# A graph transformer kernel: the first batch's rows of layers 1 and 2 picked at the end of the layer ahead, and half of its gathers dropped

## The chip, the cores and the metric

The kernel runs on one core of a Trainium2 chip. The metric is the device time of one execution in microseconds (us); lower is better. A core has a matrix engine (PE), a vector engine (DVE), a scalar engine (ACT), a general engine (POOL, which here does nothing but issue indirect gathers) and a queue engine (SP, which here issues most of the plain transfers, in the order written).

## The reference

Three layers of a graph transformer over N = 6250 nodes of width D = 64 and E = 206250 edges, which are sorted by destination node. Cut to what matters:

```python
for i in range(3):
    q = x @ Wq[i] + bq[i]; k = x @ Wk[i] + bk[i]; v = x @ Wv[i] + bv[i]
    e = edge_attr @ We[i]
    alpha = sum(q[dst] * (k[src] + e), -1) / sqrt(D)
    p = exp(alpha - segment_max(alpha, dst)[dst])
    w = p / segment_sum(p, dst)[dst]
    x = segment_sum((v[src] + e) * w[:, None], dst) + x @ Ws[i] + bs[i]
    x = relu(x)
    if i < 2: x = layer_norm(x, gamma[i], beta[i])
return layer_norm(x0 + log_softmax(x))
```

Each layer needs the row of `x` of each edge's source node, and these rows are known only when the layer ahead has finished its nodes.

## The kernel before

**Tiling.** The nodes stand in 49 blocks of 128, and the blocks in groups of four, the last two being group 44 (three blocks) and group 47 (two). The edges are cut into batches of 3072: four chunks of 768, each of six tiles of 128. There are 67 full batches and one small one; a batch is worked on as one unit, `u` = 0 to 67, and NU = 68. `chunks[layer, u].turn(j)` transposes chunk j on PE (L1754), `line.scores(u, h)` makes the scores (PE L1767, DVE maximum L1781 and L1794), `weights` the softmax weights (ACT L1800, PE L1814), `line.sums(u)` the weighted sums (PE L1826), and `line.store()` copies them out of PSUM (ACT L1833) and stores them to one of two tables `part` (SP L1839, four small transfers per unit).

**Node work.** `finish(layer, g, n)` takes a group of blocks whose sums are complete: it loads both tables' rows (`both`, L1552) and the skip term (`sk`, L1557), joins the tables (`mm` L1565, `w` L1574 and L1577, PE L1581), adds and normalises (`y` L1606, the statistics L1530 and L1532, L1545), stores the rows of the next layer's x (`x<-y`, SP L1614), and goes on in `project` to the next layer's queries and skip term (PE L1498, L1503 and L1512, DVE `skip` L1514). It is a generator: each `close_up()` moves every group in work one step on, and does a step of `reload` first, so node work lies between the edge work in the order that the program writes it. That order is the order on every engine; nothing is rearranged later.

**Source rows.** They come into `feat` in two ways. POOL gathers one tile of 128 rows per indirect transfer (`gather`, L610); in layers 1 and 2 the first batch's gathers read their indices from `src_b`, the others from a `gate`, a copy of indices on ACT (L642) that is made when a buffer has come free. Or the row is picked: PE multiplies a one-hot matrix `hot` (made on DVE from `keys`, L1382, with `which` L1371) with a resident copy `parts` of x (`Picker.batch`, L1453), DVE takes the result out of PSUM (`evacuate`: L1408 and three L1410), and ACT swaps two pieces (L1393 to L1395). The nodes stand in eight ranges for this; each is loaded through `start` (SP L1344) and split into a high and a low part (`split`: ACT cast L1315, DVE subtract L1316). Batches of layers 1 and 2 have 24 rows of tiles, of which 12 are picked and 12 gathered; picks reach ranges 0 to 5 only. `LEAD` says how many batches at a layer's start are not picked:

```python
PICKS = ((8,), (12,), (12,))
LEAD = (3, 1, 1)
```

**The end of a layer.** After the loop over u come, in writing, the last two units: turns of unit 66, its scores, `sums(65)`, a store, unit 67's turn and scores, `sums(66)`, a store, `sums(67)`, a store, with `line.refill(u)` (which hands unit u's `feat` buffer to a later batch and issues its 768 KB load of edge values, SP L579) between them. Then come the loads of keys for batches 0 to 2 of the next layer (`decode`, 384 KB each, L1913), the loads for its unit 0 (`q`, `featT`, `fourth`, `shade`), the rest of the node groups down to the store of group 47's rows, and only then the first gathers, which may read any row of x. Ranges that are not yet split follow last.

Of the kernel before, what the change touches and what calls it, by code (L numbers as in the profile page):

```python
# [11 lines left out]
F32 = mybir.dt.float32  # L12
# [9 lines left out]
P = 128  # L22
D = 64
L = 3
# [9 lines left out]
GS = 4  # L34
# [8 lines left out]
NW = 8  # L43
WT = 2
# [4 lines left out]
GC = 16  # L49
ROWS = 8  # L50
PICKS = ((8,), (12,), (12,))
LEAD = (3, 1, 1)
NH = WB // KB
AHEAD = 3

# [377 lines left out]
def main_path(  # L433
# [53 lines left out]
    nc = tc.nc  # L487
# [4 lines left out]
    REST = tiles - NT * LB * TC  # L492
    assert NT > LEAD[0] and REST <= TC
    NC = NT * LB + 1
# [31 lines left out]
    nodes = ctx.enter_context(tc.tile_pool(name="nodes", bufs=2))  # L526
# [13 lines left out]

    U0 = LEAD[0]
    STEP = -(-(N - WB * P) // (NW - 1))
# [18 lines left out]
    skS = [dram.tile([P, NB, D + 1], F32, name=f"skS{i}") for i in range(L)]  # L561
# [34 lines left out]
    def depth(n):  # L596

        return [(n // 2 + 1 - pair) // 2 for pair in range(LB // 2)]
# [32 lines left out]
    def await_turn(layer, k):  # L631

        pending.extend((layer, k, c) for c in range(batches[k][1]))
# [26 lines left out]
    for k in range(NK):  # L660
        n = min(P, NC - k * P)
# [96 lines left out]
    for k in range(NK):  # L758
        n = min(P, NC - k * P)
# [548 lines left out]
    held = []  # L1308
    lacking = []

    def split(w, y):

        at = w % HALF * WB
        here = parts[w // HALF][:, :, at : at + WB]
        nc.scalar.copy(here[:, 0], y)  # L1315
        nc.vector.tensor_tensor(here[:, 1], y, here[:, 0], ALU.subtract)  # L1316

    def range_of(layer, w):

        return xts[layer][w * STEP : w * STEP + WB * P, :].rearrange("(j p) d -> p j d", p=P)  # L1320
# [12 lines left out]

    def reload(layer):

        while held and (len(held) > 1 or not lacking):
            split(*held.pop(0))
        if not lacking:
            return
        w = lacking[0]  # L1340
        if all((layer - 1, g) in written for g, _ in groups if g * P < w * STEP + WB * P):
            lacking.pop(0)
            y = start[:, w % SLOTS * WB * D :][:, : WB * D].rearrange("p (j d) -> p j d", d=D)
            nc.sync.dma_start(y, range_of(layer, w))  # L1344
            held.append((w, y))
# [201 lines left out]
    def finish(layer, g, n):  # L1547

        at_end = g + n == NB
        both = nodes.tile([P, 2, GS, R], F32, name="both", bufs=1)  # L1550
        for h in range(2):
            nc.sync.dma_start(  # L1552
                both[:, h, :n, :],
                tables[h][g * P : (g + n) * P, :].rearrange("(j p) c -> p j c", p=P),
            )
        sk = nodes.tile([P, GS, D + 1], F32, name="sk", bufs=1)[:, :n]
        nc.sync.dma_start(sk, skS[layer][:, g : g + n, :])  # L1557
        xr = rows_of(g, n) if layer == L - 1 else None
        yield
        if not at_end and g + 2 * GS > NB:  # L1560
            for _ in range(3):
# [87 lines left out]
    def advance(those=None):  # L1649
        those = active if those is None else those  # L1650
        for g in list(those):
            if next(g, those) is those:
                those.remove(g)

    class Unit:
# [36 lines left out]
        def ask(self):  # L1692

            self.b = []
            for j in range(self.m):
                b = nc.values_load(
                    base[0:1, self.c + j : self.c + j + 1],
                    engines=(ENG.SP,),
                    min_val=0,
                    max_val=NB * P,  # L1700
                    skip_runtime_bounds_check_because="the least of a chunk's nodes, NB*128 at most",
                )
                self.b.append(b)
                nc.sync.dma_start(self.q[:, j * W : (j + 1) * W], qq[self.layer][:, ds(b, W)])
# [267 lines left out]
    def step(n=1):  # L1972
        for _ in range(n):
            advance()
# [3 lines left out]
    def close_up(n=1):  # L1978
        step(n)
        for _ in range(n):  # L1980
            advance(ending)
        if lacking or held:
            reload(current[0] + 1)
# [4 lines left out]
    serve()  # L1988
    for layer in range(L):
        line = Line(layer)  # L1990
        assert not picked(layer, 0)

        def free(u, j):
            lead = 2 * LB if not layer else min(2 * LB, LB + u)
            release(layer, u * LB + j + (0 if not layer else 1) + lead, nc.scalar.copy)

        picker = Picker(layer)
        for u in range(NU - 2):
            this = chunks[layer, u]
            picking = picker.batch(u + 1)  # L2000
            n = len(picker.picks(u + 1))
# [74 lines left out]
        more = layer + 1 < L  # L2076
# [3 lines left out]
        assert not picker.todo and not picker.hots  # L2080
        if more:
            current[0] = layer
            lacking.extend(range(NW))
            if not layer:
                early.close()
                psum.append(ctx.enter_context(tc.tile_pool(name="psum", bufs=1, space=bass.MemoryType.PSUM)))
                bank_of.update({"g": "p", "node": "a", "s1": "p", "w0": "s"})
                stock[0] = ctx.enter_context(tc.tile_pool(name="picks", bufs=2))
                parts.append(stock[0].tile([P, 2, HALF * WB, D], F32R, name="parts", bufs=1))
        u = NU - 2  # L2090
        full = chunks[layer, u]
        line.sums(u - 2)
# [23 lines left out]
        line.scores(u, 0)  # L2116
        line.scores(u, 1)
        line.sums(u - 1)
        line.refill(u - 1)
        line.store()  # L2120
        close_up()
        last.turn(0)
        last.uncode()
# [3 lines left out]
        line.scores(u + 1, 0)  # L2127
        line.scores(u + 1, 1)
        line.sums(u)
        line.refill(u)  # L2130
        line.store()
        close_up()
        line.weights(u + 1, 0)
        line.weights(u + 1, 1)
        close_up()
        line.sums(u + 1)
        line.refill(u + 1)
        line.store()
        close_up()
        if more:  # L2140
            decode(layer + 1, 0)
            decode(layer + 1, 1)
            decode(layer + 1, 2)
            ask(layer + 1, 0)
            chunks[layer + 1, 0].across()
            chunks[layer + 1, 0].shade()
# [4 lines left out]
        if more:  # L2151
            assert all((layer, g) in written for g, n in groups)
            for k in range(FB):
                if (layer + 1, k) not in loaded:
                    fetch(layer + 1, k)
                if k:
                    await_turn(layer + 1, k)
                else:
                    gather_all(layer + 1, k)
            while lacking or held:  # L2160
                reload(layer + 1)
            while ending:
                close_up()

# [44 lines left out]
```

## Time and profile before

| what | value |
|---|---|
| time, median of 3 runs | 4140.61 us (4136.73 to 4148.78) |
| the profiled execution | 4139.31 us, its span 4137.5 us |
| PE busy | 3364.6 us, 81% |
| DVE busy | 2977.8 us, 72% |
| POOL busy | 2827.9 us, 68% |
| ACT busy | 2351.6 us, 57% |
| mean granted PE clock | 0.933 |
| POOL idle between layers 0 and 1, and 1 and 2 | 59.04 us and 46.10 us |

A row of a timeline reads: start, duration (of the whole group when it has a count), engine, line and operation, output and inputs, the count, and in square brackets the idle time before it with what ended it. A row of the windows reads: the stretch, its length, busy us of PE, PE's weight loads (PEld), DVE, ACT and POOL, each with its count of instructions, then the granted PE clock, the busy share of the transfer engines and GB/s. In the rows of groups stand count, busy us, mean ns of one, and the idle time ahead of them with its releasers. "issue" is time in which an engine waited for nothing that the profile shows. SPq is SP's queue. Line numbers are those of the kernel before.

### The profile page before, as it was taken

Reading aid. Unit: us, or ns where it says so; the run is one execution under the profiler, and the core shown is the slowest. Engines: PE = TensorE matmul, PEld = TensorE weight load, DVE = VectorE, ACT = ScalarE, POOL = GpSimd, SP = SyncE. Lnnn points to the kernel's source line nnn. Section 1 sums busy time; section 2 is a strip of 40 time slices with the busy share of each in tenths; the row PEclk is TensorE's granted clock in tenths of the full one; section 3 lists DMA queues with packets and bytes.
Section 4 is the critical chain, followed back from the end, with each engine's and each line's share of the span. In section 5 each row is a group of like instructions: output and inputs, shape, how many; then the busy total and the mean of one; then the engine's idle time right before and its main releaser. Section 6 shows DMA issues by size and latency. Waiting matters only on the chain.

```text
span 4137.5 us, 105363 instructions
## 1 busy us (share of the span) xinstructions
PE 3364.6 (81%) x34183; PEld 2391.6 (58%) x34183; DVE 2977.8 (72%) x10306; ACT 2351.6 (57%) x6011; POOL 2827.9 (68%) x2774
## 2 busy tenths in 40 slices
PE   3889899999989899984778788888757878778776
PEld 1445555555555555553666666666646666666664
DVE  5677888888878888864667777777646667777775
ACT  0455565565656555563556556565635656666665
POOL 5467666666667666663777777777657777777774
PEclk9899999999999999996999999999969999999998
DMA  5667677666767666765677777777657677777774
GB/s 111 185 175 198 171 192 181 180 183 184 188 161 193 179 180 175 183 174 125 173 183 193 186 183 185 188 189 188 164 135 183 173 190 182 187 189 183 186 184 102
DMA packets 787997, 728.88 MB, mean 176 GB/s; under 512 B 487336, under 2 KB 612450, under 8 KB 787440
## 3 DMA queue, kind: packets, MB, share of 16 engines
q1 hardware_dynamic: 630436, 504.14, 47.6%
q0 software_dynamic: 88448, 90.75, 11.6%
q10 hardware_dynamic: 68556, 127.16, 8.7%
q8 instruction: 278, 4.55, 0.5%
q14 instruction: 279, 2.29, 0.2%
HBM read 562.78 MB, written 158.81 MB: 174 GB/s over the span
## 4 chain that ended last, share of the span: by engine, by line


## 5 line engine op out<-in xcount | busy, mean ns | idle before, releaser
L610 POOL DMA_INDIRECT feat<-x,gate x1592 | 1579.9, 992 | 485.4 <-issue 372.9
L610 POOL DMA_INDIRECT feat<-in_x,gate x1100 | 1175.4, 1069 | 652.6 <-ACT gate L642 323.5
L1453 PE MATMUL ps_x<-parts,hot 128*128 128x256 f32 x6336 | 941.8, 301 | 0.0
L1453 PEld LDWEIGHTS ps_x<-parts,hot 128*128 128x128 f32 x6336 | 841.8, 202 | 81.8 <-DVE feat L1410 62.5
L1757 ACT COPY featT<-ps_a 64x384 f32<-64x384 f32 x1320 | 627.1, 475 | 393.5 <-PE ps_a L1754 369.5
L1410 DVE COPY_PREDICATED feat<-which,ps_x 128x256 f32<-128x256 int32 (+1 forms) x1584 | 592.4, 374 | 54.3
L1408 DVE COPY feat<-ps_x 128x256 f32<-128x256 f32 (+1 forms) x528 | 187.7, 355 | 587.0 <-PE ps_x L1453 577.2
L1754 PE MATMUL ps_a<-ident,feat 128*128 128x128 f32 x2380 | 451.0, 289 | 176.2 <-DMA feat<-x,gate 139.7
L1101 DVE TENSOR_SCALAR hit<-ruler,pos 128x384 bf16<-128x384 f16 x1608 | 501.8, 324 | 30.3 <-PE ps_m L1121 30.2
L1754 PEld LDWEIGHTS ps_a<-ident,feat 128*128 128x128 f32 x2380 | 283.3, 144 | 385.7 <-issue 276.0
L1382 DVE TENSOR_SCALAR hot<-keys,rank 128x512 fp32r<-128x512 f16 (+1 forms) x1040 | 432.9, 482 | 9.1 <-DMA keys<-keyS 5.2
L1826 PE MATMUL ps_p<-feat,probT 128*32 128x128 f32 x6600 | 236.3, 295 | 91.4 <-ACT probT L1817 77.8
L1112 PE MATMUL ps_x<-hit,raw 128*64 128x384 bf16 x1608 | 293.8, 360 | 2.5 <-DVE hit L1101 2.2
L1112 PE MATMUL ps_x<-hit,rest 128*64 128x384 bf16 x1608 | 275.0, 338 | 0.0
L1112 PE MATMUL ps_x<-hit,end 128*64 128x384 bf16 x1608 | 274.2, 337 | 0.0
L1826 PEld LDWEIGHTS ps_p<-feat,probT 128*32 128x32 f32 x6600 | 193.6, 119 | 129.4 <-ACT probT L1817 102.9
L1767 PE MATMUL ps_s<-featT,q 128*32 128x384 f32 x1866 | 228.0, 496 | 11.6 <-DMA featT<-eaS 7.3
L1814 PE MATMUL ps_s<-ident,prob 128*128 128x128 f32 (+1 forms) x417 | 81.3, 307 | 191.6 <-ACT prob L1800 188.7
L1453 PE MATMUL ps_p<-parts,hot 128*128 128x256 f32 x992 | 163.8, 311 | 80.5 <-DVE feat L1410 73.5
L1800 ACT ACTIVATE prob<-prob,part 128x768 f32<-128x768 f32 x204 | 190.0, 931 | 68.7 <-DVE part L1794 60.1
L1453 PEld LDWEIGHTS ps_p<-parts,hot 128*128 128x128 f32 x992 | 137.1, 204 | 112.5 <-DVE feat L1410 91.8
L1833 ACT COPY part<-ps_p 128x128 f32<-128x128 f32 (+1 forms) x140 | 37.3, 267 | 244.9 <-PE ps_p L1826 239.8
(281 smaller groups left out, 5960.6 us busy)
## 6 DMA issues: line engine op xcount, KB each, us to landing
featT<-eaS SPq DMA_DIRECT2D x658, 192.0 KB
feat<-eaP SPq DMA_DIRECT2D x134, 768.0 KB
raw<-in_ea SPq DMA_DIRECT2D x536, 96.0 KB
eaS<-eT ACTq DMA_DIRECT2D x134, 384.0 KB
keys<-keyS SPq DMA_DIRECT2D x132, 384.0 KB
eaP<-feat ACTq DMA_DIRECT2D x128, 384.0 KB
shade<-maskS SPq DMA_DIRECT2D x198, 192.0 KB
fourth<-eaS SPq DMA_DIRECT2D x134, 192.0 KB
```

The source lines that it names most:

```text
L610: nc.gpsimd.indirect_dma_start(out=feat[:, c, t, 0], out_offset=None, in_=xts[layer][:, :], in_offset=bass.IndirectOffsetOnAxis(ap=index[: ...
L1101: nc.vector.tensor_scalar(hit, ruler, self.pos[:, at : at + 1], None, ALU.is_equal)
L1112: nc.tensor.matmul(self.px[j * D : (j + 1) * D, :HE], self.parts[2 * h + i].thirds[part][:, j, t * D : (t + 1) * D], self.hits[h, 2 * i + ...
L1382: nc.vector.tensor_scalar(hot[:, h], keys[self.layer, k][:, first : first + n], rank[:, h : h + 1], None, ALU.is_equal)
L1408: nc.vector.tensor_copy(found, px[:, :, :, 0])
L1410: nc.vector.copy_predicated(found, which[:, :, :, b].bitcast(I32).unsqueeze(3).to_broadcast([P, 2, m, D]), px[:, :, :, b],)
L1453: nc.tensor.matmul(px[:, t - t0, v].rearrange("p b d -> p (b d)"), hot[:, h, (2 * pair + v) * P : (2 * pair + v + 1) * P], those[:, i, b0 ...
L1754: nc.tensor.transpose(pt[:, t * P : (t + 1) * P], rows[:, 2 * t * D : 2 * (t + 1) * D], ident)
L1757: nc.scalar.copy(featT[:, :, h, :], pt[h * D : (h + 1) * D, : n * P].rearrange("d (i e) -> d i e", e=P))
L1767: nc.tensor.matmul(p_s[rows, :w], self.q[:, rows], self.featT[j][:, cols], start=True, stop=True)
L1800: nc.scalar.activation(self.prob[:n, : self.cols], self.prob[:n, : self.cols], AF.Exp, bias=neg, accum_out=self.part[:n, P + 1 : P + 2],)
L1826: nc.tensor.matmul(p_g[rows, :].rearrange("n (h d) -> n h d", h=2), self.probT[:, t, rows], batch[:, j, t], start=(t == 0), stop=(t == sel ...
```

## The change

`LEAD` becomes (3, 0, 0), so batch 0 of layers 1 and 2 is picked like the others: 12 of its 24 gathers go, and 48 pick matmuls with their hots, evacuations and swaps come in. They are made at the end of the layer ahead. The picker of the next layer is opened behind the store of unit 65's sums, which makes the first hots there; the keys of batches 0 and 1 are therefore loaded ahead of the last two units; and the picks are written out behind the store of the last sums. Of the eight ranges six are reloaded. `reload` splits at most one range per step. `refill` stands behind the stores, and the last two behind the very last store. In `finish`, `sk` is loaded ahead of `both`.

```diff
-LEAD = (3, 1, 1)
+LEAD = (3, 0, 0)
...
     def reload(layer):
-        while held and (len(held) > 1 or not lacking):
+        if held and (len(held) > 1 or not lacking):
             split(*held.pop(0))
...
     def finish(layer, g, n):
         at_end = g + n == NB
+        sk = nodes.tile([P, GS, D + 1], F32, name="sk", bufs=1)[:, :n]
+        nc.sync.dma_start(sk, skS[layer][:, g : g + n, :])
         both = nodes.tile([P, 2, GS, R], F32, name="both", bufs=1)
...
-        sk = nodes.tile([P, GS, D + 1], F32, name="sk", bufs=1)[:, :n]
-        nc.sync.dma_start(sk, skS[layer][:, g : g + n, :])
...
-        picker = Picker(layer)
+        if not layer:
+            picker = Picker(layer)
...
-            lacking.extend(range(NW))
+            lacking.extend(range(WT * max(depth(max(PICKS[layer + 1])))))
...
+            decode(layer + 1, 0)
+            decode(layer + 1, 1)
         u = NU - 2
...
         line.sums(u - 1)
+        line.store()
         line.refill(u - 1)
-        line.store()
+        if more:
+            picker = Picker(layer + 1)
+            picker.aim()
         close_up()
...
         line.sums(u)
-        line.refill(u)
         line.store()
...
         line.sums(u + 1)
-        line.refill(u + 1)
         line.store()
         close_up()
+        line.refill(u)
+        line.refill(u + 1)
         if more:
-            decode(layer + 1, 0)
-            decode(layer + 1, 1)
+            for _ in picker.batch(0):
+                pass
+            picker.flush()
             decode(layer + 1, 2)
...
-            while lacking or held:
-                reload(layer + 1)
```

Three places show how the order on the engines moves. The first is PE at the end of layer 0, between group 44's join (L1581) and its projection (L1512) and values (L1603); `hot_…` are the one-hot matrices of batch 0, one for each of three tile positions.

```order
 L1826 MATMUL ps_p<-feat,probT 32x128 x4
 L1581 MATMUL ps_a<-ident,w 128x128 x3
+L1453 MATMUL ps_x<-parts,hot_32669 128x256 x8
+L1453 MATMUL ps_x<-parts,hot_32672 128x256 x8
+L1453 MATMUL ps_x<-parts,hot_32675 128x256 x8
+L1453 MATMUL ps_x<-parts,hot_32669 128x256 x8
+L1453 MATMUL ps_x<-parts,hot_32672 128x256 x8
+L1453 MATMUL ps_x<-parts,hot_32675 128x256 x8
 L1512 MATMUL ps_a<-ws,xT 128x65 x4
 L1603 MATMUL ps_a<-ve,wT 128x64 x3
```

All 48 pick matmuls of batch 0 stand ahead of group 44's last matmuls and behind the sums of the last unit; at the end of layer 1 it is the same.

The second is DVE at the same place: behind the sixth range's split (L1316) and ahead of group 44's `skip` and `y`.

```order
 L1599 TENSOR_TENSOR vb<-vb,sk 128x192
 L1316 TENSOR_TENSOR parts<-start,parts 128x512
+L1408 COPY feat<-ps_x 128x2x128
+L1410 COPY_PREDICATED feat<-which,ps_x 128x2x128 x3
+L1408 COPY feat<-ps_x 128x2x64
+L1410 COPY_PREDICATED feat<-which,ps_x 128x2x64 x3
+L1408 COPY feat<-ps_x 128x2x128
+L1410 COPY_PREDICATED feat<-which,ps_x 128x2x128 x3
+L1382 TENSOR_SCALAR hot_32894<-keys,rank 128x512 x2
+L1382 TENSOR_SCALAR hot_32897<-keys,rank 128x512 x2
+L1408 COPY feat<-ps_x 128x2x64
+L1410 COPY_PREDICATED feat<-which,ps_x 128x2x64 x3
 L1514 TENSOR_TENSOR skip<-ps_a,sb 128x260
 L1606 SCALAR_TENSOR_TENSOR y<-ps_a,inv,vb 128x64 x3
```

Four evacuations and four hots of batch 1 stand there now. The first eight hots (six of batch 0, two of batch 1) stand further ahead on DVE, behind unit 66's maximum (L1794) and ahead of group 40's normalisation.

The third is SP at the last sums' stores and the loads of group 47 (`both`, `sk`) at the end of layer 0; the lines of `finish` have other numbers in the changed kernel.

```order
-L1344 DMA start<-x_114 128x8x64 x2
-L579 DMA feat<-eaP 128x1536
...
+L1344 DMA start<-x_114 128x8x64
 L1839 ISA
 L1839 DMA part_188<-part 32x130
 L1508 DMA qq_192<-qs 128x512
-L1552 DMA both<-part_188 128x2x130
-L1552 DMA both<-part_189 128x2x130
-L1557 DMA sk<-skS_111 128x130
-L1913 DMA keys<-keyS 128x1536 x2
+L1551 DMA sk<-skS_111 128x130
+L1555 DMA both<-part_188 128x2x130
+L1555 DMA both<-part_189 128x2x130
+L579 DMA feat<-eaP 128x1536 x2
+L1913 DMA keys<-keyS 128x1536
```

One load of a range and the `feat` load in front of the last part store go; `sk` and `both` change places; two `feat` loads and one of keys, in place of two of keys, stand behind them. The other two loads of keys stand ahead of the tail.

More of the change, by code (lines that the diff above doesn't have):

```diff
@@ L1549, in finish @@
         at_end = g + n == NB
+        sk = nodes.tile([P, GS, D + 1], F32, name="sk", bufs=1)[:, :n]
+        nc.sync.dma_start(sk, skS[layer][:, g : g + n, :])
+        xr = rows_of(g, n) if layer == L - 1 else None
         both = nodes.tile([P, 2, GS, R], F32, name="both", bufs=1)
@@ L1555, in finish @@
             )
-        sk = nodes.tile([P, GS, D + 1], F32, name="sk", bufs=1)[:, :n]
-        nc.sync.dma_start(sk, skS[layer][:, g : g + n, :])
-        xr = rows_of(g, n) if layer == L - 1 else None
         yield
@@ L1990, in main_path @@
         line = Line(layer)
-        assert not picked(layer, 0)
         def free(u, j):
@@ L2136, in main_path @@
         line.sums(u + 1)
-        line.refill(u + 1)
         line.store()
         close_up()
+        line.refill(u)
+        line.refill(u + 1)
         if more:
-            decode(layer + 1, 0)
-            decode(layer + 1, 1)
+            assert not lacking and not held
+            for _ in picker.batch(0):
+                pass
+            picker.flush()
             decode(layer + 1, 2)
```

## The prediction

> **What bounds the kernel now.** I read the page first, then the POOL rows of a middle stretch of layer 1, then the timelines around the two places where one layer ends and the next begins.
>
> ```profile
> PE 3364.6 (81%) x34183; PEld 2391.6 (58%) x34183; DVE 2977.8 (72%) x10306; ACT 2351.6 (57%) x6011; POOL 2827.9 (68%) x2774
> 2400.00:2800.00 400.00, 328.02 (x3427) 270.23 (x3426) 283.42 (x876) 240.67 (x620) 306.35 (x308) 0.95 0.73 189
> L610 POOL DMA_INDIRECT feat<-x,gate x308 | 306.7, 996 | 94.0 <-issue 72.3 <-DMA feat<-x,gate 5.8 <-DVE hot L1382 3.4
> ```
>
> By the page PE is the busiest engine (81%) and POOL has 68%. Inside layer 1 (the row of 2400 to 2800, and the POOL group of the same stretch) the reading turns: 306.7 us of gathers and 94.0 us of pauses that are nearly all "issue", together 400.7 us, fill the stretch. POOL issues one gather per 1.30 us without a break, 12 per batch; nothing else can make a unit shorter. A layer therefore lasts from its first gather through its count of gathers, plus its tail.
>
> ```profile
> 1922.18 1.46 POOL L610 DMA_INDIRECT feat<-x,src_b  x1 [59.04 <-PE ps_a L1512]
> 1938.44 0.95 POOL L610 DMA_INDIRECT feat<-x,src_b  x1 [0.30 <-issue]
> 1953.44 1.30 POOL L610 DMA_INDIRECT feat<-x,gate  x1 [0.30 <-DMA feat<-x,src_b]
> 3034.61 1.59 POOL L610 DMA_INDIRECT feat<-x,src_b  x1 [46.10 <-PE ps_a L1512]
> 3066.04 1.27 POOL L610 DMA_INDIRECT feat<-x,gate  x1 [0.30 <-DMA feat<-x,src_b]
> ```
>
> The first boundary (into layer 1) leaves POOL empty for 59.04 us, the second for 46.10. Then come the 24 gathers of batch 0, up to the first gather that reads `gate`. So the end time moves by two things only: when the first gather of a layer starts, and how many follow.
>
> **What is removed.** Twelve of batch 0's 24 gathers at each boundary. At the first, gathers 13 to 24 run from 1938.44 to 1953.44: 12 x 1.25 = 15.0 us (15.6 at the 1.30 of the middle); the second's 24 take 31.43 us in all against 31.26, so the same. They lie on the bound: -30.0 us in all.
>
> **What is paid.** The picks of batch 0 now stand in PE's and DVE's order between group 44's matmuls and its `y`, and so ahead of all of group 47, whose store the first gather waits for. The chain there, at the second boundary and then the first:
>
> ```profile
> 3016.73 0.69 DVE L1316 TENSOR_TENSOR parts<-start,parts 128x512 fp32r<-128x512 f32 x1 [3.98 <-ACT parts L1315]
> 3019.06 0.30 DVE L1532 BATCH_NORM_AGGREGATE mv<-stat 128x2 f32<-128x6 f32 x3
> 3023.30 0.17 DVE L1565 TENSOR_TENSOR mm<-sk,both 128x4 f32<-128x4 f32 x1 [3.94 <-DMA sk<-skS]
> ...
> 1902.71 0.69 DVE L1316 TENSOR_TENSOR parts<-start,parts 128x512 fp32r<-128x512 f32 x1 [4.52 <-ACT parts L1315]
> 1910.74 0.17 DVE L1565 TENSOR_TENSOR mm<-sk,both 128x4 f32<-128x4 f32 x1 [5.39 <-DMA sk<-skS]
> ```
>
> Today DVE has 3.94 and 5.39 us of idle there (a load that is waited for), and group 47's `mm` starts 5.9 and 7.3 us after the sixth split ends. The picks fill that gap and overrun it. Their pieces, from where they run today in unit 0, and in the middle of layer 1:
>
> ```profile
> 1947.41 3.75 PE L1453 MATMUL ps_x<-parts,hot 128*128 128x256 f32 x16
> 2421.67 2.12 PE L1453 MATMUL ps_x<-parts,hot 128*128 128x256 f32 x16
> 1943.59 0.29 DVE L1408 COPY feat<-ps_x 128x128 f32<-128x128 f32 x1 [5.76 <-PE ps_x L1453]
> 1943.92 0.97 DVE L1410 COPY_PREDICATED feat<-which,ps_x 128x128 f32<-128x128 int32 x3
> 1951.21 0.42 DVE L1408 COPY feat<-ps_x 128x256 f32<-128x256 f32 x1 [6.32 <-PE ps_x L1453]
> 1951.66 1.39 DVE L1410 COPY_PREDICATED feat<-which,ps_x 128x256 f32<-128x256 int32 x3
> 1952.95 1.67 DVE L1382 TENSOR_SCALAR hot<-keys,rank 128x512 fp32r<-128x512 f16 x4
> 1948.86 0.35 ACT L1393 COPY swap<-feat 64x192 f32<-64x192 f32 x1
> ```
>
> - The pick matmuls: 48, in six groups of eight. Two groups (the first 16) need no late range and run before the sixth split; the third ends beside the first evacuation. After that evacuation (1.81) frees its bank, 16 more must run before the third evacuation: 3.75 us at the clock of unit 0, 2.12 at full clock. The last group hides behind hots.
> - The DVE chain after the sixth split: first evacuation 1.81, wait for 16 matmuls 3.75 (the second evacuation, 1.26, lies inside), third 1.81, four hots of batch 1 1.67, fourth 1.26: 10.3 us; 8.7 at full clock. Then group 44's `skip` to its statistics as now, from the split's end at 3017.42 to 3019.36: 2.0. I take 10.3, since PE waits before this place.
>
> ```profile
> 3008.00:3036.00 28.00, 13.32 (x46) 9.13 (x46) 15.22 (x56) 8.99 (x17) 1.39 (x1) 0.50 0.67 183
> 1940.00:1960.00 20.00, 12.55 (x57) 9.56 (x57) 6.28 (x18) 4.81 (x14) 15.16 (x16) 0.51 0.16 28
> ```
>
> Both stretches have a granted clock of 0.50 and 0.51, the second with PE 63% busy on just such picks. The Trainium skill's page "TensorE: Matmul & The Clock Gate" (section "What's actually happening") says that the array runs at half rate by default, and at full rate once it has been busy for some 3.4 us on end. By that rule the stalls for evacuations keep the burst slow, which speaks against the change; were the burst dense enough it would turn fast midway and the sum would be some 3 us better. The trace bears out the slow case.
>
> - Hots of batch 0 and the first two of batch 1: eight at 0.42 and two `which` at about 0.2, 3.8 us on DVE, right after unit 66's maximum. They push the splits and unit 67's maximum, but DVE idles there:
>
> ```profile
> 1884.66 0.69 DVE L1316 TENSOR_TENSOR parts<-start,parts 128x512 fp32r<-128x512 f32 x1 [1.21 <-ACT parts L1315]
> 1887.41 0.69 DVE L1316 TENSOR_TENSOR parts<-start,parts 128x512 fp32r<-128x512 f32 x1 [2.07 <-ACT parts L1315]
> 2998.11 0.69 DVE L1316 TENSOR_TENSOR parts<-start,parts 128x512 fp32r<-128x512 f32 x1 [1.51 <-ACT parts L1315]
> ```
>
> At the first boundary 3.28 us of cover, so +0.5. At the second the next gap is 1.51, and more splits with waits follow it: +0.2, at most 2.3. Without any cover it would be 3.8.
>
> - SP's queue. The two `feat` loads of 768 KB leave the front of the part stores; the loads of the last ranges (`start<-x`), behind these stores, go out earlier:
>
> ```profile
> 1892.22 1.17 SPq L579 DMA_DIRECT2D feat<-eaP  x1
> 1893.64 5.01 SPq L1839 DMA_DIRECT2D part<-part  x4
> ...
> 3006.33 0.64 SPq L579 DMA_DIRECT2D feat<-eaP  x1
> 3007.55 5.29 SPq L1839 DMA_DIRECT2D part<-part  x4
> ```
>
> The issue slot (1.17; 1.22 from 3006.33 to 3007.55) plus a faster landing of the stores: the sixth split 1.9 us earlier as an estimate, between 0 (the stores wait for their sums anyhow) and 2.5 (half of the 5.0 too). `sk` ahead of `both` now: worth nothing, DVE comes later than both. Two range loads and splits fewer per boundary: off the path, nothing.
>
> - Two ACT swaps of 3 x 0.35 between the sixth cast and the table loads: +0.2, by the table loads that group 47's exponential then waits for.
> - At the first boundary only, the keys of batches 0 and 1 (768 KB) go ahead of `feat` and `featT` of the tail. There the queue is read late:
>
> ```profile
> 1877.84 0.82 PE L1767 MATMUL ps_s<-featT,q 128*32 128x384 f32 x1 [7.34 <-DMA featT<-eaS]
> 1860.00:1865.00 5.00, 4.14 (x27) 1.80 (x23) 3.73 (x11) 3.40 (x7) 2.53 (x3) 1.00 0.86 240
> 1865.00:1870.00 5.00, 4.08 (x30) 3.04 (x31) 1.71 (x7) 4.51 (x9) 0.00 (x0) 1.00 0.51 95
> ```
>
> PE waits 7.34 us for a `featT`, so a shift of the loads goes straight to the path. 768 KB at 240 GB/s is 3.2 us; the free DMA share of these two rows (0.14 and 0.49 of 5 us) is 3.15. I take +2, between 0 and 4. At the second boundary no such wait ends the tail: 0.
>
> **The sum.** Second boundary: `mm` at 3017.42 + 0.2 - 1.9 + 10.3 + 2.0 = 3028.0 against 3023.30: +4.7, +0.2 for ACT = 4.9 (bounds 2.5 and 8.9). First: 1903.40 + 0.5 - 1.9 + 12.3 = 1914.3 against 1910.74: +3.6 + 0.2 + 2 = 5.8 (1.1 and 9.7). Together +10.7 against -30.0: -19.3 us. On the profiled execution of 4139.31 us that is 4120.0; that execution lies 1.3 below the median of 4140.61 (the runs span 4136.73 to 4148.78). Its own bounds: -31.2 + 3.6 = -27.6 and -30.0 + 18.6 = -11.4, so 4112 to 4128.
>
> **Rivals.**
> 1. The picks are nearly hidden (clock full, stores much quicker, keys free): under 3 us in all are paid, -27 to -31: about 4110. For it: the 3.94 and 5.39 us of idle. Against: 10.3 us of work has to fit there.
> 2. The payment swells to 9 us or more per boundary, and the result stays within 0.3% (12.4 us, about what a measurement of this kernel can tell from no change): about 4131. It would come if the evacuations wait for PE at each of the four steps instead of one (three more times some 1.9, half of the 3.75), or if the last range lands no earlier.
> 3. The removed gathers don't shorten unit 0, because PE bounds it: about 4135 to 4140. Unit 0 holds some 19 us of PE work at half clock (6.38 in 1925 to 1940, and the 12.55 above), while POOL now takes 15. Against: batch 1's gathers need only the turn one chunk back. Turn 0 now waits for three gathers, not six, and its gate copy comes 3.0 us after the last of them:
>
> ```profile
> 1925.00:1940.00 15.00, 6.38 (x25) 5.17 (x25) 6.65 (x17) 1.44 (x4) 11.46 (x12) 0.61 0.60 144
> 1929.31 1.25 POOL L610 DMA_INDIRECT feat<-x,src_b  x1 [0.30 <-issue]
> 1933.57 0.19 ACT L642 COPY gate<-src_b 128x6 int32<-128x6 int32 x1
> ```
>
> So 6.8 us after the first gather; with all of unit 0's PE work behind it, unit 1's first turn ends at about 26, and POOL needs its release (chunk 9, at 3.75 us per chunk) at 33.75. 8 us of margin.
>
> 4. Slower. Two `feat` loads, the third keys, four `q` (16 KB), three `featT`, `fourth` and `shade` (192 KB each) now stand on SP between the last `both` and the `x` stores, which the first gather waits for: 2.9 MB.
>
> ```profile
> feat<-eaP SPq DMA_DIRECT2D x134, 768.0 KB
> keys<-keyS SPq DMA_DIRECT2D x132, 384.0 KB
> ...
> 3020.26 0.91 SPq L1552 DMA_DIRECT2D both<-part  x2
> 3029.89 2.68 SPq L1614 DMA_DIRECT2D x<-y  x2
> ```
>
> At the 183 GB/s of 3008 to 3036 they take 16 us. `both` should go at about 3014.5 (the part stores 1.9 earlier, and landing without 768 KB before them), the stores at 3029.89 + 4.9 = 3034.8: 4 us to spare. It decides against the change where these transfers hold the stores 10 to 15 us longer than that at each boundary, at some 90 GB/s; at 70 GB/s they take 41 us and the time is about 4160. Against: the lowest row here is the 95 GB/s of 1865 to 1870, where DMA was half idle.
>
> **How the numbers follow.** The forecast (4112 to 4128) has 0.60; rival 1 0.13; rivals 2 and 3 0.19 together; rival 4 and what is like it 0.08. Faster by over 0.3% (below 4128) is the forecast and rival 1, 0.73; within 0.3% 0.19; slower 0.08. The range is 4108 to 4134: it leaves out the last of rival 1, the upper half of rivals 2 and 3, and rival 4.
>
> **What would show it.** In the profile after: 12 gathers `feat<-x,src_b` per boundary, at 1.25; the first gather 5 to 6 us later than now, counted from the last gather of the layer ahead (so 65 and 51 us of POOL idle); then no POOL wait above 0.3 us through units 0 and 1. On DVE the sixth split, then some 10 us to the last evacuation, with one wait for PE of about 2.5 us inside; group 47's `mm` without a DMA wait before it. At the first boundary PE's wait for `featT` about 2 us longer. I am wrong if POOL waits for gates in unit 0, if `x<-y` waits for anything but `y`, or if PE waits for the sixth split much later than 3016.

## The result: 0.7% faster, about 29 us

The changed kernel took 4113.06 us (median of 6 runs, 4106.03 to 4118.77) against 4142.6 (6 runs, 4131.95 to 4148.78): a ratio of 0.9931, 95% interval 0.9913 to 0.9949. Its profiled execution took 4118.77 us, its span 4117.1 against 4137.5.

The POOL timeline of the changed kernel, with the last gather of layer 0, the first of layer 1 and the first that reads `gate`, and the same two at the next boundary:

```profile
1872.83 0.94 POOL L610 DMA_INDIRECT feat<-in_x,gate  x1 [0.30 <-issue]
1939.08 0.94 POOL L610 DMA_INDIRECT feat<-x,src_b  x1 [65.31 <-PE ps_a L1512]
1954.06 0.94 POOL L610 DMA_INDIRECT feat<-x,gate  x1 [0.30 <-issue]
3033.14 0.94 POOL L610 DMA_INDIRECT feat<-x,src_b  x1 [48.66 <-DMA qq<-qs]
3048.12 0.95 POOL L610 DMA_INDIRECT feat<-x,gate  x1 [0.30 <-issue]
```

POOL idles 65.31 and 48.66 us instead of 59.04 and 46.10, and batch 0's gathers take 14.98 us at both places instead of 31.26 and 31.43. The first gather comes later by 6.3 and 2.6 us, and what follows is 16.3 and 16.5 us shorter.

The span alone misleads. The last gather of layer 0 starts at 1872.83 here; in the kernel before the corresponding one started at 1862.20. The profile was 10.6 us behind before the first boundary, although in the loops of layer 0 the change only swaps the loads of `sk` and `both`. The first experiment is about that.

DVE between the sixth split and group 47's `mm`, at the second boundary:

```profile
3009.15 0.69 DVE L1316 TENSOR_TENSOR parts<-start,parts 128x512 fp32r<-128x512 f32 x1 [1.14 <-ACT parts L1315]
3009.76 0.42 DVE L1408 COPY feat<-ps_x 128x256 f32<-128x256 f32 x1
3014.88 0.42 DVE L1408 COPY feat<-ps_x 128x256 f32<-128x256 f32 x1 [2.08 <-PE ps_x L1453]
3016.64 1.67 DVE L1382 TENSOR_SCALAR hot<-keys,rank 128x512 fp32r<-128x512 f16 x4
3018.54 0.97 DVE L1410 COPY_PREDICATED feat<-which,ps_x 128x128 f32<-128x128 int32 x3
3021.36 0.17 DVE L1565 TENSOR_TENSOR mm<-sk,both 128x4 f32<-128x4 f32 x1
```

The picks' chain stands there as forecast: 9.7 us from the end of the split (3009.84) to the last evacuation (3019.51), one wait for PE inside, and `mm` 11.5 us behind the split with no wait for a load.

### The profile page after: what moved, and what is told of

It reads as the page before. It is cut to its first block, busy times and chain, and to the rows that moved or that the text cites. A ratio compares the mean times of both kernels' runs of the same rounds, so it can differ in the third digit from the quotient of the medians.

```text
span 4117.1 us, 105542 instructions
## 1 busy us (share of the span) xinstructions
PE 3376.5 (82%) x34279; PEld 2406.1 (58%) x34279; DVE 2990.8 (73%) x10348; ACT 2352.4 (57%) x6019; POOL 2802.5 (68%) x2750
## 3 DMA queue, kind: packets, MB, share of 16 engines
q1 hardware_dynamic: 626564, 503.87, 47.8%
## 4 chain that ended last, share of the span: by engine, by line
## 5 line engine op out<-in xcount | busy, mean ns | idle before, releaser
L1453 PE MATMUL ps_x<-parts,hot 128*128 128x256 f32 x6432 | 956.3, 301 | 7.0 <-DVE feat L1410 2.5
L1453 PEld LDWEIGHTS ps_x<-parts,hot 128*128 128x128 f32 x6432 | 855.6, 202 | 90.1 <-DVE feat L1410 64.3
L1410 DVE COPY_PREDICATED feat<-which,ps_x 128x256 f32<-128x256 int32 (+1 forms) x1608 | 602.1, 374 | 55.2
L1393 ACT COPY swap<-feat 64x192 f32<-64x192 f32 (+2 forms) x392 | 129.8, 331 | 93.8 <-DVE feat L1410 83.3
```

The source lines that it names most:

```text
L1410: nc.vector.copy_predicated(found, which[:, :, :, b].bitcast(I32).unsqueeze(3).to_broadcast([P, 2, m, D]), px[:, :, :, b],)
L1453: nc.tensor.matmul(px[:, t - t0, v].rearrange("p b d -> p (b d)"), hot[:, h, (2 * pair + v) * P : (2 * pair + v + 1) * P], those[:, i, b0 ...
```

## Experiments

In the table, times count from the end of the layer's last gather: unit 66's maximum (at the first boundary), the end of the sixth split, the start of group 47's `mm`, the end of its `y`, and the first gather of the next layer (POOL's idle time).

| kernel | boundary 1: maximum, split, `mm`, `y`, first gather | boundary 2: split, `mm`, `y`, first gather |
|---|---|---|
| before | 18.3, 40.3, 47.6, 56.5, 59.0 | 28.9, 34.8, 43.7, 46.1 |
| before, again | 18.6, 41.2, 47.7, 56.5, 59.1 | 29.3, 35.1, 43.9, 46.4 |
| changed | 21.7, 41.5, 53.5, 62.7, 65.3 | 25.4, 36.9, 46.2, 48.7 |
| changed, again | 20.6, 40.7, 52.9, 62.2, 64.7 | 24.0, 36.0, 45.3, 47.8 |
| changed, LEAD (3, 1, 1) | 19.8, 39.9, 41.8, 50.6, 55.5 | 25.6, 28.0, 36.9, 40.5 |
| changed, no picks of batch 0 | 21.4, 41.4, 44.8, 53.7, 56.1 | 26.2, 29.6, 38.5, 41.8 |
| changed, refills first | 21.4, 43.5, 55.3, 64.6, 67.1 | 28.3, 40.1, 49.4, 51.9 |
| picks late | 22.0, 41.6, 43.5, 52.3, 57.2 | 26.2, 28.1, 37.0, 41.3 |
| picks and refills late | 21.0, 41.5, 43.3, 52.2, 54.7 | 25.4, 27.4, 36.2, 38.9 |
| and keys late | 18.5, 38.5, 40.4, 49.2, 51.8 | 26.6, 29.5, 38.3, 41.0 |

**The changed kernel again** (no edit).

> The changed kernel once more, for a second profile and closer times. Its first profile came out 20.4 us shorter than the one before by span (4137.5 to 4117.1), but in that profile layer 0, whose edge work is not touched, was 10.7 us longer (last gather of layer 0 ends at 1873.77, before at 1863.14). Theory A: that is scatter between executions, so the true gain is nearer 30 us; then layer 0 ends here anywhere between 1860 and 1875, and the time is 4106 to 4119, 25 to 32 us under the kernel before. Theory B: the new order of the sk and both loads in layer 0 costs these 10 us; then layer 0 ends at 1873 to 1874 again. Both: POOL idle 65.3 and 48.7 us at the two boundaries within 1 us; 808 gathers of layer 1 in 1043 to 1047 us.

4111.29 us, ratio 0.9924 (0.9907 to 0.9941). Span 4102.4; layer 0's last gather ended at 1864.32, not 1873.77, and the kernel before, profiled again below, ended layer 0 at 1875.15 instead of 1863.14. Theory A: one and the same kernel ends layer 0 up to 12 us apart, while the boundaries repeat within 0.9 us. Layer 1's 808 gathers took 1042.8 us, just under the 1043 to 1047 expected. So spans of single profiles can't be compared here to better than that; stages can.

**All of the change but the picks.**

```diff
-LEAD = (3, 0, 0)
+LEAD = (3, 1, 1)
```

> The changed kernel with LEAD at (3, 1, 1): batch 0 is gathered whole again, no picks at the boundary, everything else of the change stays (orders of refill, sk, keys, six ranges). Theory A (the gathers are the gain, the picks' chain in the tail the price, and the new order alone already shortens the tail): without picks group 47's mm is gated by the loads of both, which the new order issues at 1914 and 3009 instead of 1907 (after 10.6 us more of layer 0) and 3020, so POOL idles about 56 us at the first boundary and 39 at the second, against 59 and 46 before; then 24 gathers of 31 us; time 5 to 12 us under the kernel before, 15 to 25 above the changed one. Rival: the new order alone gives nothing, boundaries of 59 and 46 us, time equal to the kernel before within 3 us. Third: the new order is the whole gain, time equal to the changed kernel.

4128.77 us, ratio 0.9961 (0.9946 to 0.9977): 9 to 22 us under the kernel before, with all 24 gathers of batch 0 back. Theory A with a larger share for the order than I had thought. The group of these gathers in the kernel before, in this one, and in the changed one:

```profile
L610 POOL DMA_INDIRECT feat<-x,src_b x48 | 48.1, 1001 | 119.2 <-PE ps_a L1512 105.1 <-issue 12.8 <-DMA feat<-x,src_b 1.2
L610 POOL DMA_INDIRECT feat<-x,src_b x48 | 45.3, 944 | 110.0 <-DMA qq<-qs 55.5 <-DVE skip L1514 40.5 <-issue 12.8
L610 POOL DMA_INDIRECT feat<-x,src_b x24 | 22.7, 944 | 120.7 <-PE ps_a L1512 65.3 <-DMA qq<-qs 48.7 <-issue 6.4
```

The idle time falls from 105.1 to 96.0 us, and one gather from 1001 to 944 ns, so that 24 take 29.97 us instead of 31.3. By stages all of the change but the picks is worth 3.5 + 5.8 + 1.3 + 1.5 = 12 us (the two idle times, then batch 0's gathers). In it group 47's `both` is loaded earlier (24.8 us after the last gather at the second boundary instead of 31.8), and `mm` with it (28.0 instead of 34.8):

```profile
3001.82 0.90 SPq L1555 DMA_DIRECT2D both<-part  x2
3005.05 0.17 DVE L1565 TENSOR_TENSOR mm<-sk,both 128x4 f32<-128x4 f32 x1
```

This run holds several edits at once: the order of refills and stores, `sk` first, six ranges instead of eight, one split per step, the keys early. Only the refills and the keys are taken apart below.

**Picks left out.** The hots are made and dropped, and POOL clears the places that the picks fill; that part of the computation is missing.

```diff
-            for _ in picker.batch(0):
-                pass
-            picker.flush()
+            nc.gpsimd.memset(loaded[layer + 1, 0][:, :, : max(picker.plan[0]), 0], 0.0)
+            for t in range(max(picker.plan[0])):
+                picker.free.append(picker.hots.pop((0, t))[0])
+            picker.which.pop(0, None)
+            picker.aim()
```

> The changed kernel with batch 0's picks left out (the places that they fill are set to zero by POOL in its idle time; that part of the computation is missing), the gathers dropped and the hots made as in the change. It shows what the boundary costs without the pick matmuls, evacuations and swaps. Theory A: POOL idle about 57 and 40 us against 65.3 and 48.7, so the picks' chain is worth 8 to 9 us at each boundary. Rival B: within 2 us of 65.3 and 48.7, the chain is hidden and something else (transfers, hots, keys) sets the boundary.

One execution: 4097.3 us. POOL, with the clearing in its idle time:

```profile
1874.97 0.76 POOL L2147 MEMSET feat<- 128x768 f32 x1
1931.05 0.95 POOL L610 DMA_INDIRECT feat<-x,src_b  x1 [55.31 <-DMA x<-y]
...
3015.13 0.95 POOL L610 DMA_INDIRECT feat<-x,src_b  x1 [41.07 <-DMA qq<-qs]
```

From the last gather it is 56.1 and 41.8 us. The picks, evacuations and swaps cost 9.0 and 6.4 us at the boundaries, theory A (8 to 9), the second a little less.

**The refills ahead of the stores again.**

```diff
         line.sums(u - 1)
+        line.refill(u - 1)
         line.store()
-        line.refill(u - 1)
...
         line.sums(u)
+        line.refill(u)
         line.store()
...
         line.sums(u + 1)
+        line.refill(u + 1)
         line.store()
         close_up()
-        line.refill(u)
-        line.refill(u + 1)
```

> The changed kernel with the refill loads (768 KB of edge values each) put back ahead of the part stores as before; picks, keys and sk stay. Theory A (with the stores first, the load of the sixth range goes out and lands earlier): the sixth split comes 3 to 4 us later than in the changed kernel at the second boundary (24.0 to 25.4 us after the last gather there, so 27.5 to 29) and 0 to 3 later at the first; with it mm of group 47, so that POOL idles 65 to 68 and 51 to 52 us. Rival B: the stores wait for their sums anyhow; splits and idle times as in the changed kernel within 1 us.

This first try, with three others, fell on a chip on which the kernel before took 5655 us and the second boundary idled 66 us, so it can be held only against kernels of the same chip, and the changed one was not among them: 80.3 and 69.6 us of idle, split at 56.5 and 46.3 us (with refills, and picks, late: 54.6 and 44.1). It was repeated where the kernel before took 4150:

> The changed kernel with the refill loads ahead of the part stores again, once more, beside a chip where the changed kernel's boundaries are known (65.3 and 64.7, 48.7 and 47.8 us of POOL idle; sixth split 41.5 and 40.7, 25.4 and 24.0 us after the last gather). Theory A (stores first lets the sixth range come earlier): sixth split 2 to 3.5 us later at both boundaries, group 47's mm 11.5 to 12.2 behind it, idle 66.5 to 68.5 and 50 to 52. Rival B: no difference over 1 us.

4113.31 us, idle 67.1 and 51.9. Sixth split and `mm` at the second boundary:

```profile
3001.74 0.69 DVE L1316 TENSOR_TENSOR parts<-start,parts 128x512 fp32r<-128x512 f32 x1 [4.07 <-ACT parts L1315]
3014.28 0.17 DVE L1565 TENSOR_TENSOR mm<-sk,both 128x4 f32<-128x4 f32 x1
```

The split waits 4.07 us, in the changed kernel 1.14, and is 3.6 us later by the table (28.3 against 24.0 and 25.4), 2.3 at the first boundary (43.5 against 40.7 and 41.5); `mm` follows 11.8 behind. Theory A: stores ahead of refills are worth 2.1 and 3.7 us with the picks in the tail. That stands on the stages of one execution; its whole time, 4113.31, is that of the changed kernel and can't show 6 us.

**The kernel before again.**

> The kernel before once more, for a second profile. In the first one its 820 gathers of layer 1 took 1066.3 us, 10.0 more than the same 820 in the changed kernel with LEAD at (3, 1, 1) (1056.3), and those of layer 2 1061.0 against 1059.7. If the 10 us are scatter of that one execution (theory A), layer 1 takes 1055 to 1062 here, and the boundaries idle 59 and 46 us within 1.5. If they belong to the kernel before (theory B: its first gathers meet loads that the change has moved), layer 1 takes 1064 to 1068 again, with the first 24 at over 31 us at both boundaries under either theory.

This was on the slow chip (5660.57 us, idle 75.0 and 66.1) and answered nothing; what it showed of the chip stands at the end. Repeated:

> The kernel before once more. The earlier repeat ran on a chip where every kernel takes some 5600 us and POOL waits for gates in the middle of the layers, so it says nothing on the 1066.3 us that layer 1's 820 gathers took in the first profile. Where the kernel takes some 4140 us: theory A (scatter of one execution) 1055 to 1062 us; theory B (it belongs to the kernel before) 1064 to 1068. Boundaries idle 59 and 46 us within 1.5 and first 24 gathers of over 31 us under both. Where it takes 5600 again, idle 75 and 66 us as in the earlier repeat.

4144.34 us; boundaries 59.1 and 46.4; layer 1 in 1061.4 us. That is within theory A, at its upper end. Without batch 0 (31.26, 31.28, 31.43 and 31.40 us) the layers take 1035.1 and 1030.1 (layer 1), 1029.6 and 1027.0 (layer 2); the changed kernel without its 14.98 takes 1030.4 and 1027.9, 1029.0 and 1027.6. One kernel differs from itself by 1.4 to 5 us there, so no gain outside batch 0 and the boundaries is shown. The tail behind the last gather of layer 2 is 2 us shorter as well (41.9 and 42.2 us before, 40.0 and 40.1 in the changed kernel), but versions whose code there is that of the changed kernel have 39.3 to 44.2, so this is not shown to be a gain either.

**Picks behind the first gathers.**

```diff
-            for _ in picker.batch(0):
-                pass
-            picker.flush()
             decode(layer + 1, 2)
...
                 else:
                     gather_all(layer + 1, k)
+            for _ in picker.batch(0):
+                pass
+            picker.flush()
             while ending:
                 close_up()
```

> The picks of batch 0 are written out behind the first gathers of the layer instead of behind the last sums, so that they are no longer ahead of group 44's and 47's node work on PE, DVE and ACT. Theory A (the picks' chain of 10 us on DVE holds group 47 up): mm of group 47 about 9 us earlier; POOL idle some 58 and 41 us against 65.3 and 48.7, bounded by the 2.9 MB of loads ahead of the x stores; unit 0's first turn waits for the picks, some 10 us behind the first gather, and POOL may then wait 0 to 3 us for a gate. Time 8 to 15 us under the changed kernel. Rival B (the transfers behind both hold the x stores): idle stays within 2 us of 65.3 and 48.7 and the time within 4 us. Rival C: the late picks make POOL wait for gates by as much as was won; time within 4 us, with POOL waits of over 5 us in unit 0 or 1.

4097.89 us, ratio 0.9886 (0.9867 to 0.9904), some 13 us under the changed kernel of the same set. Theory A: idle 57.2 and 41.3, as without picks.

```profile
1932.66 0.94 POOL L610 DMA_INDIRECT feat<-x,src_b  x1 [57.22 <-DVE skip L1514]
1945.88 0.20 ACT L642 COPY gate<-src_b 128x6 int32<-128x6 int32 x1
...
1927.17 0.62 DVE L1545 TENSOR_TENSOR y<-y,gb 128x128 f32<-128x128 f32 x2
1928.13 0.98 SPq L1614 DMA_DIRECT2D x<-y  x2
```

Unit 0's first gate copy comes 13.2 us after the first gather, and POOL waits for none of them: the picks lie wholly under the gathers. `y` ends at 1927.79, and the first gather follows 4.9 us later, in the changed kernel 2.6. There the same two rows are:

```profile
1935.88 0.62 DVE L1545 TENSOR_TENSOR y<-y,gb 128x128 f32<-128x128 f32 x2
1929.95 6.95 SPq L1614 DMA_DIRECT2D x<-y  x2
```

SP has issued the store of group 47's rows (the second of the two) 0.4 us after `y` in the changed kernel, at 1936.90, and 1.3 us after it here, at 1929.11. So 0.9 us of the 2.3 us pass before the store is issued, and the rest behind its issue.

**The last two refills late as well.**

```diff
-        line.refill(u)
-        line.refill(u + 1)
         if more:
...
             assert all((layer, g) in written for g, n in groups)
+            line.refill(u)
+            line.refill(u + 1)
```

> The picks behind the first gathers (as in the run before that did this) and, besides, the last two refill loads (1.5 MB) behind the x stores and the first gathers. There the first gather came 4.9 and 4.3 us after the last y, against 2.6 and 2.5 in the changed kernel. Theory A (the x store lands late because it queues behind these loads): 2.5 us again at both boundaries, POOL idle about 55 and 39.5 us, time 2 to 6 us under that run (4097.9), if the two refills, needed first in units 2 and 3, are still in time. Rival B: the rest of the loads (keys, featT, fourth, shade) are enough to delay it: idle 57 and 41. Rival C: the refills come too late and POOL or the sums wait in units 2 and 3.

The slow chip: 5622.85 us against 5654.68, ratio 0.9937 (0.9913 to 0.996); first gather 2.5 and 2.6 us after `y`. Repeated:

> Picks and the last two refills behind the first gathers, once more. On the slow chip the first gather came 2.5 us after the last y, so the two refills alone had held the x store up. Theory A, where the kernel before takes some 4140 us: 2.5 us here too (4.9 and 4.3 with the refills ahead), POOL idle 54 to 56 and 39 to 40 us, no wait of POOL over 0.3 us in layers 1 and 2; time 4090 to 4098, ratio 0.987 to 0.989. Rival: idle as with the refills ahead, 57 and 41. Where the kernel before takes 5600 us, ratio 0.994 again.

4097.62 us, ratio 0.9894 (0.9879 to 0.9909). `y` to first gather is 2.5 and 2.7 us, idle 54.7 and 38.9, so the two refills had delayed the store. But the time did not move:

```profile
1933.42 0.94 POOL L610 DMA_INDIRECT feat<-x,src_b  x1 [54.71 <-DMA qq<-qs]
1949.58 0.94 POOL L610 DMA_INDIRECT feat<-x,gate  x1 [1.19 <-ACT gate L642]
```

POOL waits 1.19 us (and 1.6 at the second boundary) for batch 1's first gate, against the expectation that no wait would come. Of the 2.5 and 2.4 us won at the boundaries, that gives back half to two thirds; the rest is below what these runs tell apart. It also shows how little the picks had to spare under the gathers in the run before.

**The keys late too.** `decode(layer + 1, 0)` and `(layer + 1, 1)` move from ahead of unit 66 to behind its scores.

> The same as the run with the two refills behind the first gathers, and besides the keys of batches 0 and 1 loaded behind the last featT of the layer instead of ahead of the last two units. Theory A (at the first boundary these 768 KB delay the featT that PE waits for): unit 66's maximum at 18 to 19 us after the last gather instead of 20.6 to 22.0, and POOL idle 2 to 3.5 us less at the first boundary than in that run, the same within 1 us at the second; time 2 to 4 us less. Rival B: featT waits for something else, no change at the first boundary. Rival C: the hots now wait for the keys, and the loss is the same or more.

The slow chip: 5620.06 us, ratio 0.9936; idle 67.8 and 59.8 against 67.9 and 57.5. Rival B there. Repeated:

> The same with the keys of batches 0 and 1 behind the last featT. On the slow chip the first boundary did not change (unit 66's maximum 34.5 against 34.8 us) and the second became 2.3 us longer. Theory A (the keys delay featT where the kernel takes some 4140 us: there unit 66's maximum came at 18.3 and 18.6 us in the kernel before, at 20.6 to 22.0 with both keys ahead and at 19.8 with one): maximum at 18 to 19.5 us and POOL idle 1 to 3 us less at the first boundary than in the run beside it. Rival B: maximum stays at 20.5 to 22, the keys are not the cause.

4095.35 us, ratio 0.9892 (0.9873 to 0.9911). PE's wait for the tail's `featT`, with the keys ahead (the run above) and behind:

```profile
1887.03 0.81 PE L1767 MATMUL ps_s<-featT,q 128*32 128x384 f32 x2 [0.93 <-DMA featT<-eaS]
1896.11 0.82 PE L1767 MATMUL ps_s<-featT,q 128*32 128x384 f32 x1 [8.27 <-DMA featT<-eaS]
...
1883.80 0.82 PE L1767 MATMUL ps_s<-featT,q 128*32 128x384 f32 x1 [7.46 <-DMA featT<-eaS]
```

With the keys behind, the first of these two waits is gone and the other 0.8 us shorter. Unit 66's maximum comes at 18.5 us instead of 21.0, as in the kernel before, and the first boundary is 2.9 us shorter. The second is 2.1 longer: its sixth split comes 1.2 us later, and `mm` then waits 0.91 us for `both`. So the sum is the same time. Theory A for the first boundary; a version that moves the keys there alone was not tried.

The best times are those with the picks late, about 1.1% under the kernel before.

## Why the prediction held, point by point

4120.0 was forecast, 4113.06 and 4111.29 were measured. With the stages of two profiles of each kernel:

| term | forecast | measured |
|---|---|---|
| gathers of batch 0, both boundaries | -30.0 | -32.7 (31.3 and 31.4 to 15.0) |
| first boundary | +5.8 | +6.0 (59.1 to 65.0) |
| second boundary | +4.9 | +2.0 (46.3 to 48.2) |
| sum | -19.3 | -24.7 |

The times say -29.5 and -32.6 us, with intervals of -21 to -36 and -24 to -39. Both hold the -24.7, the second barely; whether something more was won outside the boundaries and batch 0 is open.

The time alone does not tell the forecast from its rival 1 (the picks nearly hidden, about 4110): 4113.06 and 4111.29 lie nearer to that, and the second just under the forecast's own bounds of 4112 to 4128. The stages do: 8.0 us are paid at the boundaries, not under 3, and the picks' chain stands open on DVE. The result came out lower than 4120 because two other terms, the gathers and SP's queue, were put too small, and because of some 5 to 8 us that no stage accounts for.

- **What bounds.** Held: POOL has no wait over 0.3 us from the first gather of layer 1 into layer 2 but the boundary itself. Rival 3 (PE bounds unit 0) fell with the same row of waits, and more so with the picks late, where PE has all of them in unit 0 and POOL still does not wait (1.2 to 1.6 us where the first gather came earlier still).
- **Gathers.** Twelve at 1.25 was a little small. The first twelve of the kernel before took 16.3, the last twelve 15.0, and the twelve that are left take 14.98: the slow ones vanished, not the plain ones. With all 24 in the new order they take 29.97, so this belongs to the rest of the change, not to the picks. The traces show what stands beside the slow gathers in the kernel before:

```profile
1925.19 1.32 POOL L610 DMA_INDIRECT feat<-x,src_b  x1 [0.30 <-issue]
1922.14 0.67 DVE L1316 TENSOR_TENSOR parts<-start,parts 128x512 fp32r<-128x512 f32 x1
1925.00 0.69 DVE L1316 TENSOR_TENSOR parts<-start,parts 128x512 fp32r<-128x512 f32 x1 [2.19 <-ACT parts L1315]
1928.24 2.59 DVE L1382 TENSOR_SCALAR hot<-keys,rank 128x512 fp32r<-128x512 f16 x6
```

The gathers at 1922.18 (1.46 us), 1925.19 (1.32) and 1929.31 (1.25) run while DVE does the seventh and the eighth split and batch 1's hots. Over the whole of layer 1 there, 110 of the 133 gathers of more than 1.0 us overlap such a split or hot, and 44 of the other 687. In the changed kernel, and in the version with `LEAD` (3, 1, 1), the two splits are gone and the first hots stand ahead of the first gather. No run tested this link by itself.
- **The chain of the picks.** `mm` was to follow the split by 12.3 us: 11.9 and 12.2, 11.5 and 12.0. The one wait for PE was to be about 2.5 us: 2.50 and 2.08, and 2.75 and 2.56 in the second profile. It was half right on the clock:

```profile
1910.00:1914.00 4.00, 2.91 (x23) 2.71 (x23) 2.31 (x9) 0.79 (x4) 0.00 (x0) 1.00 0.53 143
1914.00:1917.00 3.00, 1.01 (x4) 0.60 (x4) 2.29 (x6) 0.58 (x1) 0.00 (x0) 0.98 0.65 141
1917.00:1919.00 2.00, 1.79 (x8) 1.82 (x9) 1.15 (x5) 0.68 (x2) 0.00 (x0) 0.50 0.92 344
1919.00:1922.00 3.00, 3.00 (x22) 2.87 (x20) 1.17 (x3) 0.37 (x2) 0.00 (x0) 0.78 0.98 373
1917.21 4.46 PE L1453 MATMUL ps_x<-parts,hot 128*128 128x256 f32 x24 [1.23 <-DVE feat L1410]
```

The first 24 picks ran at full clock (1.00, and 0.98 in 1914 to 1917). Then, after pauses of 1.45, 0.34 and 1.23 us with four picks between them, the last 24 began at 0.50, and their burst took 4.46 us: more than at full clock (3.2 by 2.12 for 16), less than at half (5.6 by 3.75). The third evacuation waits for the first 16 of them, and these came within 3.6 us here (1917.21 to 1920.76) and 3.1 to 3.8 us at the other three places, against the 3.75 of the forecast: nearer to half clock than to full (2.12), since the clock came back mostly behind them. The Trainium skill's page "TensorE: Matmul & The Clock Gate" (section "What's actually happening") has the clock come back after a busy window of about 3.4 us, and the trace agrees: 0.50 at the start of a burst of 4.46 us, 0.78 in the stretch of its end. For the fall the page names an idle window of the same length; here the clock fell although no pause of PE in that stretch was over 1.45 us.
- **SP's queue: the mis-sized term.** The sixth split was to come 1.9 us earlier. At the second boundary it came 4.4 earlier in all (29.1 to 24.7), 3.6 of it by the refills alone. I had bounded it by the issue slot and half a store's wait, 2.5; the 768 KB ahead of the stores delayed what is behind them by more. At the first boundary the refills gave 2.3.
- **Hots.** +0.5 and +0.2. From unit 66's maximum to unit 67's it takes 8.3 and 8.2 us with them at the first boundary, against 7.8 twice; 8.5 twice against 8.2 twice at the second: +0.5 and +0.3.
- **Keys.** +2 at the first boundary: 2.7 by unit 66's maximum (18.42 to 21.17 in the mean), and the last run takes it back to 18.5. The sign given for it was half right: PE's wait for `featT` grew from 7.34 and 7.58 us to 8.63 and 8.58, not by 2. One thing in the text on the kernel before is put right here: it loads the keys of batches 1 and 2 at a boundary, not of 0 to 2, since batch 0 has no picks there; the changed kernel loads 384 KB more.
- **ACT's swaps.** +0.2 behind `mm`; from `mm` to the end of `y` it takes 9.3 us instead of 8.9 at both boundaries, +0.4. Whether the swaps are the cause was not separated.
- **`sk` first.** Costed at nothing; not separated.
- **Slower (rival 4).** The loads behind `both` did reach the x store once the tail was short: 4.9 and 4.3 us from `y` to the gather instead of 2.5, as soon as the picks no longer stood ahead. In the changed kernel they had drained in time, as forecast: 2.6 and 2.5. The prediction called the 95 GB/s of 1865 to 1870 the lowest row there; its own row of 1940 to 1960 has 28, at a DMA share of 0.16, so that argument was weaker than it read.

The forecast was within 9 us because the picks in the tail cost what was worked out. But it read the change as gathers against picks, and the runs split it otherwise: the rest of the change (the order of stores and loads, the ranges left out) is worth some 12 us by itself, and on top of it the picks save 15 + 15 us and cost 9.5 + 7.7. Put behind the gathers, they cost 1.7 + 0.8.

## What to carry to other kernels

Where one engine is saturated through a stage, count its instructions there and time its idle spans between stages; here they added up to 24.7 us of an effect of some 30, and the idle spans repeat within 1 us where whole times scatter by 10. Work that replaces part of a saturated engine's load belongs where that engine is already running, not in the chain that lets it start: the same picks cost 17 us ahead of the first gather and about 2.5 behind it. Look at what stands ahead of small stores in a queue that issues in order: loads of 768 KB there, moved behind them, gave 2.1 and 3.7 us at the two boundaries, by the stages of one execution.

## What was not expected of the hardware

One of the chips ran every kernel in some 5650 us. Layers there are not bound by POOL; the kernel before, its gathers, and a stretch of layer 1:

```profile
L610 POOL DMA_INDIRECT feat<-x,gate x1592 | 1540.5, 968 | 1424.6 <-ACT gate L642 924.2 <-issue 410.2 <-DVE feat L1410 78.7
3300.00:3700.00 400.00, 279.50 (x2420) 218.39 (x2419) 201.70 (x626) 168.27 (x431) 207.93 (x213) 0.82 0.52 130
```

POOL waits 924.2 us for gates, and the granted clock is 0.82 where it was 0.95 in the middle of a layer. A gather itself is no slower (968 ns against 992). The two versions with late picks that ran there still won 0.6% (0.9937, 0.9913 to 0.996, and 0.9936, 0.9913 to 0.9958), against 1.1% elsewhere. In both, POOL waits 9.6 us for batch 1's first gate at each boundary: there the late picks do not lie under the gathers. The version with the picks in the tail and the refills first took nearly the same time (5625.9 us, one execution against 5622.85 and 5620.06), so that putting the picks late pays is shown for the other chips only. Why that chip is slower was not looked into.
